# Cross-attention block: order of the first loads, products of the unit matrix at the start, and keys and scaling in the first unit

## The chip, the cores and the metric

The kernel runs on one core of one Trainium2 chip. The metric is the device time of one execution in microseconds (us). Before the change it is 1689.89 us, the median of three runs that lie between 1689.68 and 1690.12. One more execution was recorded with the profile; all durations below come from it.

## The reference

Three residual blocks on x (8 x 64 rows of 512). Only the first one is touched. It is a cross-attention from x to a context of 8 batches x 1601 keys x 256:

```python
q = (layernorm(x) @ Wq).reshape(B, Sq, 16, 128)    # Wq 512 x 2048
k = (ctx @ Wk).reshape(B, Skv, 16, 128)            # Wk 256 x 2048
v = (ctx @ Wv).reshape(B, Skv, 16, 128)
q, k = rmsnorm(q, gq), rmsnorm(k, gk)              # over each head's 128
attn = softmax(einsum('bqhd,bkhd->bhqk', q, k) / sqrt(128))
x = x + einsum('bhqk,bkhd->bqhd', attn, v).reshape(B, Sq, 2048) @ Wo
```

Behind it come a causal self-attention and a feed-forward block with ternary weights.

## The kernel before

**Scores without stored keys.** The scores are not computed from keys that lie in memory. Wk is folded into the queries: for each head a = Wk_h^T (q gq gk) is made once (`a_sb`), so a score is a product of the raw context with a. The root of each key's mean square (its rmsnorm) is still needed, and for that the keys are computed, squared and summed, but not kept. Every product on TensorE (PE) is in fp32, and a matmul instruction of fp32 shows as two records in the profile.

**Units and steps.** There are 16 units u = (b, g): 8 batches, 2 groups of 8 heads. A batch's 1601 keys are 12 tiles of 128 and a rest of 65, the *tail*. `step(u, q)` handles two tiles, q = 0 to 5. The key product of two tiles and the score product are each made from seven block products instead of eight (the names p_u, p_5, p_2 and c12, c22, c11 belong to the keys' blocks, s_a and s_2 to the scores'). The order on PE, VectorE (DVE), ScalarE (ACT) and GpSimd (POOL) is the order in which the Python code calls them; only SyncE's transfers are placed by a scheduler. In one step:

- p_u (a11 b11), copied to p1 by ACT (L917); then the early part of tail work, if any; then the scaling of the step before (`later`, L931-932); in q5 the tail's scores sp (L633);
- p_5 and s_a, copied to p5 and half (L944, L951); p_u again, copied to u2 (L956); p_5 again; c12 = p_5 + u2 on DVE (L963) and its four squares with sums on ACT (`squares`, L684);
- on DVE a transpose of the next context blocks (`transpose_context`, L194) (in unit 0 in steps q1 to q4); on ACT and DVE some work on the feed-forward weights (L597 to L612);
- `product_7`: p_u a third time and c22 = p_u + p5 on DVE (L981), its squares on ACT;
- two s_a, DVE's sum L1006, p_2, c11 (L1010) and its squares; the late part of the tail work; the fourth p_u product (a22 n4), which adds onto the bank that c22 has read, and its squares on ACT; s_2 and the last s_a.

`scale_pair` is put into `later` at the end of a step: Ln and Exp on ACT (L104, L105: the root of sixteen sums), a DVE product that scales the 128 x 1024 scores (L654), and DVE's running maxima (L668, L670; one for the first pair of tiles, two for each other pair).

From u = 1 on, a step also holds the softmax and the value products of the unit before (`weigh`, L775), which unit 0 does not have.

**Tails.** All 8 x 65 tail keys are laid side by side in `cxP` and cut into five tiles. `tail_roots` / `key_roots` (L260 to L290) make their key products kp (L266, two halves of 4 heads for each tile and group; each half is two matmuls 128x512), squares on ACT (L274), sums on DVE (L275), and the root; then small DMAs put it in its place. For g = 0 this is done at the very start, for g = 1 in unit 0: one tile in each of q0 to q3, a half early and a half late in the step (the fifth tile's roots are made before).

**The start.** `load_tails` (L252 to L257) loads the tails in four pairs of batches, 133 KB each: b0-1 and b4-5 on SyncE's queue, b2-3 and b6-7 on ScalarE's. Then SyncE's queue loads the first half of Wk for g = 0 (524 KB; columns 0 to 511 of both row blocks, L301), its second half, x in four tiles (262 KB each, L312), Wq and the rest; ScalarE's queue loads gq and gk (L315, L316). POOL makes the unit matrix `ident`. PE turns the tails of four batches by transposes (`turn_tails`, L507), then makes kp with Wk's first half for each tile, the second halves, the turned rows of x, the queries (`two_heads`) and a. Unit 0 begins at 126.69 us.

Of the kernel before, what the change touches and what calls it, by code (L numbers as in the profile page):

```python
# [1 line left out]

# [7 lines left out]
F32 = mybir.dt.float32  # L10
# [9 lines left out]
P = 128  # L20
# [8 lines left out]
def perceiver_kernel(  # L29
# [18 lines left out]
    nc = tc.nc  # L48
# [3 lines left out]
    HD = gq.shape[0]  # L52
# [3 lines left out]
    HG = H // G  # L56
# [3 lines left out]
    NC = C // P  # L60
    NJ = (KV + P - 1) // P
    TAIL = KV - (NJ - 1) * P
# [15 lines left out]
    const = ctx.enter_context(tc.tile_pool(name="const", bufs=1))  # L78
# [5 lines left out]
    ident = const.tile([P, P], F32, name="ident")  # L84
# [61 lines left out]
    wk_sb = [wkv.tile([P, NC, HG * HD], F32, tag="w", name=f"wk{g}") for g in range(G)]  # L146
# [100 lines left out]
    cxP = const.tile([P, NC, B, TAIL], F32, name="cxP")  # L247
    krP = const.tile([P, B, H], F32, name="krP")

    def load_tails(qp):  # L250
        t = qp.tile([P, B, C], F32, tag="wq3", name="cxt")
        for b in range(0, B, 2):  # L252
            (nc.scalar if b % 4 else nc.sync).dma_start(
                t[:TAIL, b : b + 2], cx[b : b + 2, NJF * P :, :].rearrange("b k c -> k b c")
            )
        return t

    def key_roots(ct, g, kr, new_kp, new_ksq):


        r = kr.shape[0]
        ssq = small.tile([P, HG], F32, tag="ssq", name="ssq", bufs=5)
        for p in range(HG // 4):
            kp = new_kp()
            for c in range(NC):
                nc.tensor.matmul(  # L266
                    kp[:r].rearrange("p h d -> p (h d)"),
                    ct(c),
                    wk_sb[g][:, c, ts(p, 4 * HD)],
                    start=(c == 0),  # L270
                    stop=(c == NC - 1),
                )
            ksq = new_ksq()
            nc.scalar.activation(ksq[:r], kp[:r], AF.Square)  # L274
            nc.vector.tensor_reduce(ssq[:r, ts(p, 4)], ksq[:r], AX.X, ALU.add)  # L275
            yield
        rsqrt_into(kr, ssq[:r], 1.0 / HD, eps_t)

    def tail_roots(i, g, new_kp, new_ksq):

        flat = cxP.rearrange("p c b k -> p c (b k)")
        n0, n1 = i * P, min((i + 1) * P, B * TAIL)
        kr = small.tile([P, HG], F32, tag="krt", name="krt", bufs=5)[: n1 - n0]
        yield from key_roots(lambda c: flat[:, c, n0:n1], g, kr, new_kp, new_ksq)

        for b in range(B):
            a, e = max(n0, b * TAIL), min(n1, (b + 1) * TAIL)
            if a < e:
                nc.sync.dma_start(
                    krP[a - b * TAIL : e - b * TAIL, b, ts(g, HG)], kr[a - n0 : e - n0, :]  # L290
                )

    n_tails = (B * TAIL + P - 1) // P
    with tc.tile_pool(name="qphase", bufs=1) as qp, tc.tile_pool(
        name="qps", bufs=2, space=PSUM
    ) as ps:
        cxt = load_tails(qp)

        def load_wk(g, p):
            cols = slice(4 * HD * p, 4 * HD * (p + 1))  # L300
            nc.sync.dma_start(  # L301
                wk_sb[g][:, :, cols],
                wk[:, g * HG * HD : (g + 1) * HG * HD][:, cols].rearrange(
                    "(c p) n -> p c n", p=P
                ),
            )

        for p in range(HG // 4):
            load_wk(0, p)
        x_sb = qp.tile([P, NTT, D], F32, tag="x_sb", name="x_sb")  # L310
        for t in range(NTT):
            nc.sync.dma_start(x_sb[:, t, :], xf[ts(t, P), :])  # L312
        gq_t = const.tile([P, 1], F32, name="gq_t")
        gk_t = const.tile([P, 1], F32, name="gk_t")
        nc.scalar.dma_start(gq_t, gq.rearrange("(p o) -> p o", o=1))  # L315
        nc.scalar.dma_start(gk_t, gk.rearrange("(p o) -> p o", o=1))  # L316
        wq_sb = []

        def load_wq(i):
# [12 lines left out]
            load_blocks(0, q)  # L332

        xT = qp.tile([P, ND, NT], F32, name="xT_q")
        gqk = const.tile([P, 1], F32, name="gqk")
        wkT, qraw, qr = {}, {}, {}

        def transpose_wk(h):
# [150 lines left out]
        with tc.manual_schedule(  # L489
            engines={  # L490
                mybir.EngineType.PE,
                mybir.EngineType.DVE,
                mybir.EngineType.Activation,
            }
        ):

            roots = [
                tail_roots(i, 0, new_kp, new_ksq_) for i in range(n_tails)
            ]
            xns_q = []  # L500

            def turn_tails(n):
                nonlocal n_b
                while n_b < n:
                    tp = ps.tile([P, NC, P], F32, tag="q", name="tp_cx", bufs=3)
                    for c in range(NC):
                        nc.tensor.transpose(  # L507
                            tp[:, c, :TAIL],
                            cxt[:TAIL, n_b, ts(c, P)],
                            ident[:TAIL, :TAIL],  # L510
                        )
                    (nc.scalar.copy if n_b % 2 else nc.vector.tensor_copy)(
                        cxP[:, :, n_b, :], tp[:, :, :TAIL]
                    )
                    n_b += 1


            ends = [-(-min((i + 1) * P, B * TAIL) // TAIL) for i in range(n_tails)]
            n_b = 0
            turn_tails(ends[0] + 2)  # L520
            mvs = []
            for i in range(n_tails):
                if i == 2:
                    mvs = [moments(x_sb, t) for t in range(2)]
                    xns_q = [normalise(x_sb, t, qp, mvs[t]) for t in range(2)]
                next(roots[i])
                turn_tails(min(ends[min(i + 1, n_tails - 1)] + 2, B))
            nc.vector.scalar_tensor_tensor(
                gqk, gq_t, float(HD) ** -0.5, gk_t, ALU.mult, ALU.mult
            )  # L530
            load_wq(3)
            for i in range(n_tails):
                if i == NTT:
                    row_sums()
                next(roots[i], None)
                if i < NTT:
                    tp = ps.tile([P, ND, P], F32, tag="tp", name="tp_ln")
                    for c in range(ND):
                        nc.tensor.transpose(tp[:, c, :], xns_q[i][:, ts(c, P)], ident)
                    nc.scalar.copy(xT[:, :, ts(i, P)], tp)  # L540
                    if i + 2 < NTT:
                        xns_q.append(normalise(x_sb, i + 2, qp))
                    next(roots[i], None)
            head_sums(0)
            for n in range(H // 2 + 1):
                if n + 1 < H // 2:
                    head_sums(n + 1)
                two_heads(n)
                if n == 0:
                    next(roots[NTT], None)  # L550
                if n == HG // 2:
                    weight_sums(0)
                    transpose_context(0, 0)

    ps = ctx.enter_context(
        tc.tile_pool(name="ps", bufs=2, space=PSUM, reuse_waits="tile")
    )
# [124 lines left out]
    def squares(ssq, half, k):  # L682
        for h in range(4):
            nc.scalar.activation(  # L684
                k[:, ts(h, HD)],
                k[:, ts(h, HD)],
                AF.Square,
                accum_out=ssq[:, 4 * half + h : 4 * half + h + 1],
            )
# [190 lines left out]
    later = []  # L880

    def weigh(k):
        nonlocal n_av
        for _ in range(k):
# [4 lines left out]
                    finish(n_av // NJ)  # L889
            n_av += 1  # L890

    def step(u, q):
        nonlocal n_tp, n_q, wv_sb
        b, g = divmod(u, G)
# [23 lines left out]
        roots = iter(())  # L918
        if u > 0:
            weigh(1)  # L920
        elif q < n_tails - 1:
            roots = tail_roots(
                q,
                1,
                lambda: ps.tile([P, 4, HD], F32, tag=f"y{q % 2}", name="kp", bufs=1),
                new_ksq,
            )
            next(roots)
        for js in probs[1:]:
            less_max(u - 1, js)  # L930
        while later:  # L931
            later.pop(0)()

        n_early = 1 if q == 4 else 0
# [27 lines left out]
        c12 = kept("c12")  # L962
        nc.vector.tensor_tensor(c12, p_5, u2, ALU.add)  # L963
        squares(ssq[:, 0], 1, c12)
        for js in probs[n_early + 1 :]:
            exponentials(u - 1, js)
        if probs:
# [69 lines left out]
            scale_scores(u, q, s, kr)  # L1037

        later.append(scale_pair)
        if u == 0 and q == n_tails - 2:  # L1040
            weight_sums(1)
        if q == NQU - 1 and u < last:
            query_sums(u + 1)
# [278 lines left out]
    with tc.manual_schedule(engines={mybir.EngineType.PE}):  # L1322
# [115 lines left out]
        o = own_projection(2)  # L1438
# [13 lines left out]
        o = own_projection(3)  # L1452
# [63 lines left out]
        for t in range(NTT):  # L1516
            op = ps.tile([P, D], F32, tag="m", name="fop")
            y = t2([P, D], "fy")

            n_parts = 2 if t == NTT - 1 else 1  # L1520
            for part in range(n_parts):
                cols = ts(part, D // n_parts)
                for r in range(NF):
# [3 lines left out]
                    for n_ in range(2):  # L1527
# [4 lines left out]
                            start=(r == 0 and n_ == 0),  # L1532
                            stop=(r == NF - 1 and n_ == 1),
                        )
                if t == 0:
                    ss = ps.tile([P, NTT], F32, tag="y0", name="ss", bufs=1)
                    for k in range(NTT):
# [4 lines left out]
                            start=True,  # L1542
                            stop=True,
# [55 lines left out]
```

## Time and profile before

| what | us |
|---|---|
| median of three runs | 1689.89 |
| profiled execution | 1689.57 |
| its span, first to last instruction | 1687.8 |
| PE busy in the span | 1668.6 |
| DVE, ACT, POOL busy | 1194.6, 1155.2, 448.1 |
| first record of PE / first kp | 3.77 / 9.60 |
| unit 0, steps q0 to q5 | 126.69 to 199.96 |

The profile is that of one execution on the chip. Its page gives the busy time of each engine, and "the chain that ended last", which is followed back from the last instruction: at each step to what released it. Besides, the trace can be asked for the waits of an engine (who waited for whom, how long), for the timeline of an engine (start, duration, engine, line, operation, tiles, number of records taken together; in brackets the idle time before it and what ended it), and for windows of time (busy time of each engine, the granted clock, the share of the DMA engines that was busy, and GB/s). Matmuls are pipelined: the spacing of the records, not the duration of one, says what a product costs PE. A 128x512 product of fp32 follows the next after 0.86 us in the full-speed parts of the trace.

### The profile page before, as it was taken

What the parts mean: (1) busy time and instruction counts of PE and PEld (TensorE: products, weight loads), DVE (VectorE), ACT (ScalarE), POOL (GpSimd) and SP (SyncE); (2) the same over time, 40 slices, a digit from 0 to 9 for tenths busy, and PEclk for the clock granted to TensorE, in tenths of its full rate; (3) what the DMA queues carried; (4) which work ended last, traced back from release to release, by engine and by line L of the source; (5) the groups of instructions that cost most, each with busy time, mean ns of one, the idle gap of its engine ahead of it and who ended that gap; (6) DMA issues with size and microseconds to landing.
All of it is one profiled execution on the core that took longest, in us unless ns stands there. A gap on an engine that the chain in (4) does not pass through costs nothing.

```text
span 1687.8 us, 20130 instructions
## 1 busy us (share of the span) xinstructions
PE 1668.6 (99%) x5472; PEld 953.1 (56%) x5472; DVE 1194.6 (71%) x1918; ACT 1155.2 (68%) x4511; POOL 448.1 (27%) x590
## 2 busy tenths in 40 slices
PE   7999899999999999999999999999999999999999
PEld 4665455555555555555555555555555554466787
DVE  4446878787888778787878787878788786245541
ACT  4667787878787877777777878787878773023441
POOL 3211232324232323232322323242324122100040
PEclk9999999999999999999999999999999999999999
DMA  6001122212221222222222222121221216500330
GB/s 200 16 0 36 33 52 45 48 39 50 49 52 36 45 47 49 48 43 47 43 49 47 44 46 47 40 57 43 46 43 37 63 30 238 156 1 1 100 101 25
DMA packets 255977, 92.61 MB, mean 55 GB/s; under 512 B 210144, under 2 KB 236536, under 8 KB 255864
## 3 DMA queue, kind: packets, MB, share of 16 engines
q1 hardware_dynamic: 246426, 69.04, 18.3%
q0 software_dynamic: 8864, 22.02, 4.4%
q8 instruction: 43, 0.70, 0.2%
q14 instruction: 70, 0.57, 0.1%
q10 hardware_dynamic: 574, 0.27, 0.1%
HBM read 77.62 MB, written 7.34 MB: 50 GB/s over the span
## 4 chain that ended last, share of the span: by engine, by line
PE 94%; ACT 3%; DVE 2%; DMA 1%; issue 0%; SPq 0%; DVEq 0%; ACTq 0%
PE y L775 21%; PE p_u L680 19%; PE s_a L680 14%; PE p L680 14%; PE gu L1414 4%; PE op L861 3%; PE s L680 2%; PE fop L1528 2%; PE mm_qk L1209 2%; PE aps L484 2%; PE vp L846 2%; PE sp L633 2%; PE q_u L388 2%; PE kp L266 1%; PE q L388 1%; ACT c L684 1%
## 5 line engine op out<-in xcount | busy, mean ns | idle before, releaser
L684 ACT ACTIVATE c<-c 128x128 f32<-128x128 f32 x1152 | 340.6, 297 | 143.4 <-DVE c L981 57.7
L775 PE MATMUL y<-s,cxn 128*128 128x512 f32 x768 | 356.6, 592 | 0.0
L775 PEld LDWEIGHTS y<-s,cxn 128*128 128x128 f32 x768 | 144.6, 190 | 151.2 <-issue 137.0
L684 ACT ACTIVATION_READ_ACCUMULATOR c<-c 128x1 f32 x1152 | 215.4, 187 | 0.0
L762 POOL TENSOR_TENSOR den<-den,s 128x512 f32<-128x512 f32 x150 | 190.7, 1271 | 43.4 <-ACT s L753 36.4
L680 PEld LDWEIGHTS s_a<-aT,cxS 128*128 128x128 f32 x576 | 109.3, 190 | 138.0 <-issue 126.8
L969 POOL COPY gate<-mx 128x1 f32<-128x1 f32 x60 | 11.0, 183 | 619.0 <-DVE mx L668 287.6
L680 PE MATMUL s_a<-aT,cxS 128*128 128x256 f32 x576 | 171.4, 379 | 0.0
L654 DVE TENSOR_TENSOR s<-s,ssq 128x1024 f32<-128x1024 f32 x96 | 117.2, 1221 | 25.4 <-ACT ssq L105 25.3
L753 ACT ACTIVATE s<-s,zero_t 128x1024 f32<-128x1024 f32 (+1 forms) x117 | 115.9, 991 | 4.6 <-DVE s L749 4.6
L670 DVE TENSOR_TENSOR mx<-mx,s 128x512 f32<-128x512 f32 x160 | 113.6, 710 | 7.5
L749 DVE TENSOR_TENSOR s<-s,mB 128x1024 f32<-128x1024 f32 (+1 forms) x117 | 116.4, 1017 | 2.2 <-ACT mB L727 2.1
L981 DVE TENSOR_TENSOR c<-p_u,p 128x512 f32<-128x512 f32 x96 | 64.9, 676 | 71.6 <-PE p_u L680 71.6
L1006 DVE TENSOR_TENSOR s<-s_a,half 128x512 f32<-128x512 f32 x96 | 66.1, 688 | 58.1 <-POOL den L762 40.7
L684 ACT ACTIVATE p_u<-p_u 128x128 f32<-128x128 f32 x384 | 99.9, 260 | 9.4
L680 PE MATMUL p_u<-wkS,cxT 128*128 128x512 f32 x192 | 98.7, 595 | 2.3 <-DVE c L981 2.3
L680 PE MATMUL p_u<-wkS,cxS 128*128 128x512 f32 x192 | 98.3, 594 | 1.5 <-ACT p L917 1.5
L680 PE MATMUL p<-wk,cxS 128*128 128x512 f32 x192 | 98.4, 594 | 0.0
L680 PE MATMUL p<-wkS,cxS 128*128 128x512 f32 x192 | 98.1, 592 | 0.0
L680 PE MATMUL p<-wk,cxT 128*128 128x512 f32 x192 | 98.0, 592 | 0.0
L680 PE MATMUL p_u<-wk,cxS 128*128 128x512 f32 x192 | 98.0, 592 | 0.0
L680 PE MATMUL p_u<-wk,cxT 128*128 128x512 f32 x192 | 98.0, 592 | 0.0
(232 smaller groups left out, 3248.4 us busy)
## 6 DMA issues: line engine op xcount, KB each, us to landing
cxn<-in_ctx_dram SPq DMA_DIRECT2D x192, 128.0 KB
cxB<-in_ctx_dram SPq DMA_DIRECT2D x192, 64.0 KB
wf<-in_L_ffn_w_gate_up_dram SPq DMA_DIRECT2D x32, 256.0 KB
fgu<-fw POOLq DMA_DIRECT2D x4, 2048.0 KB, 8.9
fw<-wT SPq DMA_DIRECT2D x192, 32.0 KB
wq<-in_L_xattn_Wq_dram SPq DMA_DIRECT2D x4, 1024.0 KB
wf<-in_L_ffn_w_proj_dram SPq DMA_DIRECT2D x16, 256.0 KB
wo<-in_L_xattn_Wo_dram POOLq DMA_DIRECT2D x16, 256.0 KB, 6.9
```

Of the source, the lines that this page charges most:

```text
L388: nc.tensor.matmul(out_, a[:, c], b[:, c], start=first, stop=True, skip_group_check=not first)
L654: nc.vector.tensor_tensor(flat, flat, kr.unsqueeze(2).to_broadcast([P, 2 * HG, S]), ALU.mult)
L670: nc.vector.tensor_tensor(mx[u][:r], mx[u][:r], s[:r], ALU.max)
L680: nc.tensor.matmul(out_, a, w, start=start, stop=True, skip_group_check=not start)
L684: nc.scalar.activation(k[:, ts(h, HD)], k[:, ts(h, HD)], AF.Square, accum_out=ssq[:, 4 * half + h : 4 * half + h + 1],)
L749: nc.vector.tensor_tensor(t, t, m.to_broadcast([r, len(js), W]), ALU.subtract)
L753: nc.scalar.activation(t, t, AF.Exp, bias=zero_t[: t.shape[0]], scale=1.0)
L762: eng.tensor_tensor(den[u][:r], den[u][:r], s[:r], ALU.add)
L775: nc.tensor.matmul(yps[u][c], cxn[u, j][:r, ts(c, P)], s[:r], start=(j == 0), stop=(j == NJ - 1),)
L981: nc.vector.tensor_tensor(c22, p_u, p5, ALU.add)
L1006: nc.vector.tensor_tensor(quarters[:, 1::2], s_a, half[:, 0:2], ALU.add)
L1414: nc.tensor.matmul(gu[:, cols], fgu_sb[rr // 8][:, rr % 8, c, :], xs_[n_][c][:, cols], start=(c == 0 and n_ == 0), stop=(c == ND - 1 and n ...
```

## The change

It has three parts.

1. *First loads.* SyncE's queue now starts with tails b0-1, Wk's first row block (columns 0 to 511), tails b4-5; ScalarE's with tails b2-3, Wk's second row block, tails b6-7. The other half of Wk is loaded as before by L301's line, but DVE first writes one column of its place (a copy out of tail b2-3, a memset and two small copies), and the load has to wait for these writes; on SyncE it now stands behind the first three tiles of x. gq and gk are loaded through POOL's queue; gq's load stands between the two instructions that make the unit matrix.
2. *Unit-matrix products.* PE multiplies the unit matrix with itself three times (128x256) before the first transposes of the tails and three times after them. Their result is not used.
3. *Unit 0.* The tail keys of g = 1 are handed out in halves from one chain over the four tiles: q0, q1 and q4 take two (early and late), q2 and q3 one (early), q5 none. In unit 0 alone, the scaling of the step before is called behind c12 and its squares, instead of ahead of p_5. The sums of Wk's blocks for g = 1 (`weight_sums(1)` on POOL) move from the end of q3 to the end of q4.

```diff
     def load_tails(qp):
         t = qp.tile([P, B, C], F32, tag="wq3", name="cxt")
         for b in range(0, B, 2):
-            (nc.scalar if b % 4 else nc.sync).dma_start(
+            q = nc.scalar if b % 4 else nc.sync
+            q.dma_start(
                 t[:TAIL, b : b + 2], cx[b : b + 2, NJF * P :, :].rearrange("b k c -> k b c")
             )
+            if b < 4:
+                c = b // 2
+                q.dma_start(wk_sb[0][:, c, 0 : 4 * HD], wk[ts(c, P), 0 : 4 * HD])
+        nc.vector.tensor_copy(gqk[:TAIL], t[:TAIL, 3, 0:1])
+        nc.vector.memset(gqk, 0.0)
+        for c in range(NC):
+            nc.vector.tensor_copy(wk_sb[0][:, c, 4 * HD : 4 * HD + 1], gqk)
         return t
...
-        for p in range(HG // 4):
-            load_wk(0, p)
+        load_wk(0, 1)
...
-        nc.scalar.dma_start(gq_t, gq.rearrange("(p o) -> p o", o=1))
-        nc.scalar.dma_start(gk_t, gk.rearrange("(p o) -> p o", o=1))
+        nc.gpsimd.dma_start(gq_t, gq.rearrange("(p o) -> p o", o=1))
+        nc.gpsimd.dma_start(gk_t, gk.rearrange("(p o) -> p o", o=1))
...
+            idle = ps.tile([P, 2, P], F32, tag="ss", name="idle", bufs=1)
+            def idle_products(n):
+                for _ in range(n):
+                    nc.tensor.matmul(
+                        idle, ident, ident.unsqueeze(1).to_broadcast([P, 2, P]),
+                        start=True, stop=True,
+                    )
+            idle_products(3)
             turn_tails(ends[0] + 2)
+            idle_products(3)
...
+    roots_1 = itertools.chain(
+        *(tail_roots(i, 1, new_y, new_ksq) for i in range(n_tails - 1))
+    )
     def step(u, q):
...
-        elif q < n_tails - 1:
-            roots = tail_roots(
-                q,
-                1,
-                lambda: ps.tile([P, 4, HD], F32, tag=f"y{q % 2}", name="kp", bufs=1),
-                new_ksq,
-            )
-            next(roots)
+        elif q < n_tails:
+            roots = itertools.islice(roots_1, 0 if q in (2, 3) else 1 if q < 2 else None)
+            next(roots_1)
...
-        while later:
+        while later and u > 0:
             later.pop(0)()
...
         nc.vector.tensor_tensor(c12, p_5, u2, ALU.add)
         squares(ssq[:, 0], 1, c12)
+        while later:
+            later.pop(0)()
...
-        if u == 0 and q == n_tails - 2:
+        if u == 0 and q == n_tails - 1:
             weight_sums(1)
```

More of the change, by code (lines that the diff above doesn't have):

```diff
@@ L1 @@
+import itertools
 from contextlib import ExitStack
@@ L248, in perceiver_kernel @@
     krP = const.tile([P, B, H], F32, name="krP")
+    gqk = const.tile([P, 1], F32, name="gqk")
     def load_tails(qp):
@@ L334, in perceiver_kernel @@
         xT = qp.tile([P, ND, NT], F32, name="xT_q")
-        gqk = const.tile([P, 1], F32, name="gqk")
         wkT, qraw, qr = {}, {}, {}
@@ L519, in perceiver_kernel @@
             n_b = 0
+            idle = ps.tile([P, 2, P], F32, tag="ss", name="idle", bufs=1)
+            def idle_products(n):
+                for _ in range(n):
+                    nc.tensor.matmul(
+                        idle,
+                        ident,
+                        ident.unsqueeze(1).to_broadcast([P, 2, P]),
+                        start=True,
+                        stop=True,
+                    )
+            idle_products(3)
             turn_tails(ends[0] + 2)
+            idle_products(3)
             mvs = []
@@ L890, in weigh, with new_y @@
             n_av += 1
+    n_y = 0
+    def new_y():
+        nonlocal n_y
+        n_y += 1
+        return ps.tile([P, 4, HD], F32, tag=f"y{n_y % 2}", name="kp", bufs=1)
+    roots_1 = itertools.chain(
+        *(tail_roots(i, 1, new_y, new_ksq) for i in range(n_tails - 1))
+    )
     def step(u, q):
```

## The prediction

> **What bounds the kernel now.** I read the engine totals and the chain first, then TensorE's waits up to 200 us (the start and unit 0 of the attention, the only places the change touches), then the timelines there.
>
> ```profile
> span 1687.8 us, 20130 instructions
> PE 1668.6 (99%) x5472; PEld 953.1 (56%) x5472; DVE 1194.6 (71%) x1918; ACT 1155.2 (68%) x4511; POOL 448.1 (27%) x590
> PE 94%; ACT 3%; DVE 2%; DMA 1%; issue 0%; SPq 0%; DVEq 0%; ACTq 0%
> ```
>
> TensorE (PE) is busy all but 19 us: the time changes by PE's gaps, by work added to PE, and by PE running at a lower clock. Nothing else counts.
>
> ```profile
> PE kp L266 <- DMA wk<-in_L_xattn_Wk_dram: 4.5, 1, 4.5
> PE tp_cx L507 <- DMA cxt<-in_ctx_dram: 3.8, 1, 3.8
> PE p_u L680 <- DVE c L981: 1.9, 2, 1.3
> PE p_u L680 <- ACT p L917: 0.6, 1, 0.6
> ```
>
> Two groups of gaps: 8.3 us before the first key product (columns: sum, times, longest), and in unit 0 small ones, most on c22 (L981). PE's timeline of the start shows a third cost, a slow clock:
>
> ```profile
> 3.77 1.32 PE L507 MATMUL tp_cx<-ident,cxt 65*128 65x65 f32 x8 [3.77 <-DMA cxt<-in_ctx_dram]
> 9.60 3.65 PE L266 MATMUL kp<-wk,cxP 128*128 128x512 f32 x4 [4.50 <-DMA wk<-in_L_xattn_Wk_dram]
> ...
> 13.33 1.93 PE L266 MATMUL kp<-wk,cxP 128*128 128x512 f32 x4
> ```
>
> A matmul of fp32 is two records. The same four take 3.65 us at 9.60 and 1.93 at 13.33 (the last record's tail of about 0.2 included): half speed until about 13.0, which is 3.4 us after PE's steady work began. From 13.08 PE has 1.4 us of gaps up to unit 0 at 126.69, so what the start gains is carried almost rigidly.
>
> **The start.** The change brings half of Wk's first half to both queues behind two key pairs, not four. Before, PE needs the 1056 KB of tails and first Wk piece; after, cxt 0 to 3 and the two Wk pieces, 266 + 524 = 790 KB. The transfers are what limits:
>
> ```profile
> 2.00:4.00 2.00, 0.23 (x2) 0.26 (x3) 0.00 (x0) 0.04 (x1) 0.00 (x0) 1.00 0.86 233
> 6.00:8.00 2.00, 0.00 (x0) 0.00 (x0) 0.00 (x0) 0.00 (x0) 0.00 (x0) 1.00 0.80 249
> ```
>
> (last two columns: share of the DMA engines, GB/s). At 233 to 258 GB/s from 2 us on, 790 KB are there at 5.3 us. The first Wk piece lay ready on most engines at 6.8 though PE waited until 9.60: by the completion records two engines ended 2 to 2.7 us after the rest. So the halves come between 5.3 and 6.6, or with the same laggards at 7.7 to 9.0. The later loads are not due: second Wk half at 21.4, x at 16.7, each landed 5 us or more before; holding one by a DVE write costs PE nothing, though if the hold reached past 18 us PE would wait there one for one. On SP the held load stands before x's fourth tile and the Wq loads; Wq's sums are used at 34.3. The four tiny DVE writes stand before the copies of tp_cx and wait for cxt 2-3, which tp_cx waits for too (landed by 4.0).
>
> gq and gk go from ACT's queue to POOL's, and gq's issue stands ahead of the unit matrix's last step. Such an issue on POOL takes
>
> ```profile
> 1398.05 0.54 POOL L840 DMA_DIRECT2D wo<-in_L_xattn_Wo_dram  x1 [0.67 <-PE y L775]
> 1412.21 0.76 POOL L1096 DMA_DIRECT2D wa_qk<-in_L_attn_w_attn_dram  x1 [13.63 <-DVE o_h L857]
> ```
>
> so ident is ready at 1.9 to 2.4 us instead of 1.32 (1.03 + 0.29). PE then runs three unit products 128x256: each half of a cold 128x512 matmul of 2 x 0.854 us (spacing of the records at 9.60), so 3 x 0.854 = 2.56, to 4.5-5.0; transposes 0.9 to 1.1 (1.32 for eight records at the same clock, less where it rises), to 5.5-6.0. The clock rises 3.4 us after 1.9-2.4, i.e. at 5.3-5.8, so the last three products take 1.29 (warm; to 6.8-7.3) or 2.56 (cold; to 8.1-8.6). Key products start when both are done: 6.8 to 9.0; I take 7.9, the middle. They take 4 x 0.43 = 1.72 warm, ending at 9.6, where before the next work began at 13.08: **-3.5 us**. Bounds: start 6.8 warm gives 8.5, -4.6; start 9.0 cold gives 9.0 + 3.4 = 12.4, -0.7.
>
> The Trainium skill, "TensorE: Matmul & The Clock Gate", section "Part 1: The HAM clock gate (the 'warmup' mystery)", says that the window of about 3.4 us runs free and doesn't start with the kernel's work; the row above, 3.4 us, fits a start on its edge. By that rule the warm clock could come up to one window later than I take, and some of the gain with it. The skill's "DMA: Bandwidth & Descriptors", section "Issuing engines are not separate DMA queues", speaks against loading by two queues: it says this saves issue time only. The 0.80 to 0.94 shares agree that the engines are the limit; here what comes first changes, not the rate, so by rule and by row the gain is that of order alone.
>
> **Unit 0, keys.** The eight halves of L266 (1.72 us each) are only spread anew: two in q0, q1 and q4, one in q2 and q3; before two in q0 to q3. PE's work stays: six steps of 9.03 plus 9 x 1.72 (sp included) = 69.7 us. Before the steps took 12.46, 12.46, 12.47, 12.64, 10.82, 12.42 = 73.3, so 3.6 us of stalls, in q4 and q5:
>
> ```profile
> 185.71 1.12 PE L680 MATMUL p_u<-wkS,cxT 128*128 128x512 f32 x2 [0.54 <-DVE c L981]
> 198.13 1.12 PE L680 MATMUL p_u<-wkS,cxT 128*128 128x512 f32 x2 [1.32 <-DVE c L981]
> ```
>
> That is the product a22*n4, which adds onto the bank that c22 reads. Spreading keys alone would help q4.
>
> **Unit 0, scaling.** Before, the scaling of step q-1 (two ACT steps, a DVE product of 1.22, one or two maxima, one in q1) runs early in step q. After it stands behind c12 and its squares: ahead of cxT and of **c22 on DVE**, and ahead of c22's squares on ACT. DVE in step q1 (from 139.15) before:
>
> ```profile
> 143.59 1.22 DVE L654 TENSOR_TENSOR s<-s,ssq 128x1024 f32<-128x1024 f32 x1
> 144.84 0.69 DVE L668 TENSOR_TENSOR mx<-s 128x512 f32<-128x512 f32 x1
> 145.45 0.68 DVE L963 TENSOR_TENSOR c<-p,u 128x512 f32<-128x512 f32 x1
> 146.05 0.70 DVE L194 STREAM_TRANSPOSE cxT<-cxB 128x512 f32<-128x512 f32 x1
> 146.67 0.67 DVE L981 TENSOR_TENSOR c<-p_u,p 128x512 f32<-128x512 f32 x1
> ```
>
> c12 keeps its time, since PE up to there is unchanged. Its four squares run on ACT from 146.17 to 147.38, offsets 7.02 to 8.22. Then Ln and Exp:
>
> ```profile
> 142.82 0.33 ACT L104 ACTIVATE ssq<-ssq,eps_t 128x16 f32<-128x16 f32 x1
> 143.18 0.31 ACT L105 ACTIVATE ssq<-ssq,zero_t 128x16 f32<-128x16 f32 x1
> ```
>
> 0.67 together, to 8.89; scaling from 8.99 to 10.2; a maximum to 10.9, a second to 11.6; cxT to 12.25 (one maximum to 11.55); c22 to 12.9 (12.2). PE reaches a22*n4 at 9.03, or at 10.75 with a late key half before it (early half or sp included). So it stalls: q0 nothing (no scaling yet), q1 12.2 - 10.75 = 1.4, q2 and q3 3.9 each, q4 12.9 - 10.75 = 2.2, q5 3.2 (no cxT; up to 4.2, since DVE work beside POOL was slower there, the scaling 1.57 against 1.22). Steps: 12.5, 13.9, 14.65, 14.65, 14.6, 13.95 = 84.2, **+11.0** on 73.3. The first step of unit 1 has 1.8 us of stalls on the same chain; its scaling stays early, I take 0.5 back. The moved sums on POOL (one step later) are first used in unit 1. Bounds for the unit: +8 if DVE's and ACT's steps overlap more than in these rows or the transposes hide, +12.5 with POOL's slowdown in q4 and q5.
>
> **Sum.** 1689.57 (profiled execution; span 1687.8, 1.8 lie around it) + 11.0 - 0.5 - 3.5 = 1696.6; the median, 1689.89, stands 0.3 above it, so **1696.9 us**.
>
> **Rivals.**
> - (a) *c22 doesn't bind*: in the rows c22 is done at 8.2 and wanted at 9.03 or 10.75, and the start gain stands. If moving the scaling delays c22 by less than 0.8 us (DVE not blocked by the wait for ACT), keys in halves also remove the 3.6 us: 1689.57 - 3.5 - 3.6 = 1682.5. Against: engines run in order, and c22 comes after the scaling in program order. 7%.
> - (b) *The start pays for a smaller loss*: -4.6 and +6 to +8, 1691 to 1693. 10%.
> - (c) *No gain at the start*: the loads behind (x on SP is issued without a wait) share the engines, the laggards stay, ident is late: 1689.57 + 10.5 = 1700.1. 14%.
> - (d) *Unit products don't raise the clock* (the change doesn't do what it says): key products at 7.9 take 3.4, end 11.3, -1.8: 1698.3. 11%.
> - My forecast: 58%.
>
> About 0.2% (3.4 us) can be told from no change here. Faster: (a), 0.07. Same: (b) and a small tail of the forecast, 0.11. Slower: 0.82. Range 1691.0 to 1701.5: from (b) with both best bounds to +12.5 with -0.7.
>
> **What would show it.** Right: PE's waits up to 200 us list c22 (L1017 now) with about 14 us in five of unit 0's six steps, q2 and q3 the longest near 3.9; DVE shows scaling between c12 and c22 in unit 0; kp begins near 7.9 with four records in 1.9 us; unit 0 begins near 123.2. Wrong: step q2 of about 10.8 us (then (a)), first kp records of 3.6 us (d), or kp at 9.6 again (c).

## The result, and the profile after

The changed kernel takes 1702.54 us (median of four runs, 1700.53 to 1704.03), against 1690.01 before: 1.0078 times, interval 1.0066 to 1.0090. It is slower, as forecast, but by 12.5 us instead of 7.0, and it lies outside the range. The execution with the profile took 1700.53, the least of the four: its span, PE's busy time and the waits of PE up to 230 us (columns: sum, times, longest):

```profile
span 1698.7 us, 20159 instructions
PE 1674.5 (99%) x5484; PEld 957.5 (56%) x5484; DVE 1195.8 (70%) x1922; ACT 1156.6 (68%) x4511; POOL 448.5 (26%) x592
```

```profile
PE p_u L707 <- DVE c L1017: 14.0, 6, 3.6
PE idle L537 <- POOL ident masks.py:199: 2.5, 1, 2.5
```

The two waits for transfers at the start (8.3 us) have become one of 2.5 us for the unit matrix; the waits for c22 have grown from 2.3 (three of them up to 230 us) to 14.0 us. PE is busy 5.9 us longer. The six added products take some 4.2 of it (2.46 to 5.18 and 6.26 to 7.72), the first key products give back 1.8, and 3.5 are left: part of PE's work ran slower. PE's timeline of the start:

```profile
2.46 2.93 PE L537 MATMUL idle<-ident 128*128 128x256 f32 x6 [2.46 <-POOL ident masks.py:199]
5.18 1.29 PE L519 MATMUL tp_cx<-ident,cxt 65*128 65x65 f32 x8
6.26 1.62 PE L537 MATMUL idle<-ident 128*128 128x256 f32 x6
7.72 1.88 PE L280 MATMUL kp<-wk,cxP 128*128 128x512 f32 x4
```

Key products begin at 7.72 instead of 9.60 and take 1.88 instead of 3.65. Unit 0 begins at 122.98 instead of 126.69: 3.71 us gained. It ends at 210.92 and takes 87.94 instead of 73.27: 14.67 lost. The difference, 10.96, is all of the profiled execution's loss. PE's wait for c22 in q1 to q5, with the wait in brackets:

```profile
147.87 1.12 PE L707 MATMUL p_u<-wkS,cxT 128*128 128x512 f32 x2 [1.52 <-DVE c L1017]
...
162.48 1.12 PE L707 MATMUL p_u<-wkS,cxT 128*128 128x512 f32 x2 [3.60 <-DVE c L1017]
...
178.79 1.12 PE L707 MATMUL p_u<-wkS,cxT 128*128 128x512 f32 x2 [3.60 <-DVE c L1017]
...
193.39 1.30 PE L707 MATMUL p_u<-wkS,cxT 128*128 128x512 f32 x2 [1.88 <-DVE c L1017]
...
209.10 1.12 PE L707 MATMUL p_u<-wkS,cxT 128*128 128x512 f32 x2 [3.00 <-DVE c L1017]
```

They are 1.5, 3.6, 3.6, 1.9, 3.0 = 13.6 us (the sixth wait is in unit 1), where the forecast had 1.4, 3.9, 3.9, 2.2, 3.2. And DVE in q2 shows why, as the walk had it: c12, then 1.9 us idle for the root, the scaling, two maxima, the transpose, and only then c22:

```profile
155.98 0.69 DVE L997 TENSOR_TENSOR c<-p,u 128x512 f32<-128x512 f32 x1 [1.20 <-PE p L707]
158.55 1.22 DVE L681 TENSOR_TENSOR s<-s,ssq 128x1024 f32<-128x1024 f32 x1 [1.88 <-ACT ssq L106]
159.81 1.42 DVE L697 TENSOR_TENSOR mx<-mx,s 128x512 f32<-128x512 f32 x2
161.15 0.70 DVE L195 STREAM_TRANSPOSE cxT<-cxB 128x512 f32<-128x512 f32 x1
161.77 0.65 DVE L1017 TENSOR_TENSOR c<-p_u,p 128x512 f32<-128x512 f32 x1
```

Waits of 13.6 us on 69.7 of work make 83.3; unit 0 took 87.94. What is missing stands in the clock. Windows of 3.41 us, laid from the moment at which PE's clock first rose, 6.48 us (columns that matter: window, its length and PE's busy time; PEclk is the number before the last two):

```profile
160.08:163.49 3.41, 1.01 (x3) 0.53 (x4) 3.38 (x6) 1.03 (x7) 1.48 (x4) 1.00 0.32 81
163.49:166.91 3.42, 3.42 (x8) 2.03 (x7) 2.45 (x7) 3.10 (x19) 0.26 (x1) 0.50 0.47 75
...
173.73:177.14 3.41, 1.46 (x5) 0.57 (x3) 2.21 (x3) 1.06 (x6) 0.00 (x0) 1.00 0.00 0
177.14:180.56 3.42, 1.77 (x6) 1.22 (x7) 2.97 (x6) 1.79 (x12) 1.74 (x4) 1.00 0.20 32
...
190.80:194.21 3.41, 1.53 (x4) 0.49 (x3) 3.38 (x6) 0.84 (x6) 1.29 (x4) 1.00 0.28 77
194.21:197.62 3.41, 3.41 (x7) 1.87 (x6) 1.58 (x4) 2.62 (x15) 3.33 (x4) 0.50 0.49 77
```

Twice a window in which PE was busy for 1.0 or 1.5 us is followed by a whole window at half clock. Each costs up to 1.7 us: 3.4 together; the rest is some 0.25 us around each wait, which the waits' list doesn't count (the records' ends are modelled, and the first product behind a wait takes 0.1 longer). The first of the two falls behind a wait of 3.6 us, the second behind one of 1.88 us only, while the other wait of 3.6 us (175.2 to 178.8) is cut in two by the windows' edge and brings nothing on. In the four runs the mean clock is 0.998, 0.997, 0.997 and 0.996, in the order of their times but for 0.6 us between the two at 0.997: each 0.001 is 1.7 us, one window at half clock. So the number of such windows varies, by these means from two to four. That this alone spreads the times isn't shown: the kernel before has a clock of 1.000 in every run and still spreads from 1686.77 to 1690.92 (16 runs beside e1 to e4), and in e4 the lowest clock, 0.996, stands beside the shortest time.

### The profile page after: what moved, and what is told of

Its sections match the earlier page's. It is cut to its first block, busy times and chain, and to the rows that moved or that the text cites. A ratio compares the mean times of both kernels' runs of the same rounds, so it can differ in the third digit from the quotient of the medians.

```text
span 1698.7 us, 20159 instructions
## 1 busy us (share of the span) xinstructions
PE 1674.5 (99%) x5484; PEld 957.5 (56%) x5484; DVE 1195.8 (70%) x1922; ACT 1156.6 (68%) x4511; POOL 448.5 (26%) x592
## 4 chain that ended last, share of the span: by engine, by line
PE 94%; ACT 2%; DVE 2%; issue 0%; DMA 0%; POOL 0%; DVEq 0%; POOLq 0%
PE y L802 20%; PE p_u L707 19%; PE s_a L707 14%; PE p L707 14%; PE gu L1450 4%; PE op L888 3%; PE s L707 2%; PE fop L1564 2%; PE mm_qk L1245 2%; PE aps L496 2%; PE vp L873 2%; PE sp L660 2%; PE q_u L400 2%; PE kp L280 1%; PE q L400 1%; PE bp L111 1%
```

## The theories

**Theory 1.** The scaling behind c12 delays c22, because DVE works in order; the waits this makes on PE cost their own length and, where they leave a window nearly empty, half clock for the next one. The start and the keys in halves are gains that stand. **Rivals:** the keys in halves or POOL's moved sums bear part of the loss; the low clock has another source; late scaling costs wherever it is put; the start's gain comes from the unit products and not from the loads. All times below have the same kernel before beside them (medians 1689.83, 1689.16 and 1689.87 in three groups: e1 to e4, e5 to e8, e9 to e11). The second group ran on another chip, so runs of different groups are compared by how far each lies from its own group's median.

## The experiments

**e1: scaling early again.** In the changed kernel:

```diff
-        while later and u > 0:
+        while later:
             later.pop(0)()
...
         squares(ssq[:, 0], 1, c12)
-        while later:
-            later.pop(0)()
```

> The changed kernel, but with unit 0's scaling in its old place (ahead of p_5); loads, unit products and keys in halves stay. Theory 1 (the whole loss is made by the scaling behind c12: 14.0 us of waits for c22, and two or more stretches of 3.4 us at half clock that these waits bring on): no waits for c22 in q1 to q4, clock 1.000 from the start's end on, 1690.0 - 3.7 at the start - 1.5 to 3.5 in unit 0 = 1683 to 1685. Rival (keys in halves or POOL's later sums carry part of the loss): above 1687.

Measured: 1684.99 us, ratio 0.9971 (0.9960 to 0.9983), clock 1.000; waits for c22 0.8 us in all, the other waits of unit 0 small:

```profile
PE p_u L707 <- DVE c L1015: 0.8, 2, 0.4
```

The place of the scaling alone is worth 1702.54 - 1684.99 = 17.5 us; the rest of the change is a gain of 4.8. The rival about keys and POOL's sums falls.

**e2: the waits filled.** PE gets work that nobody reads, where it would wait:

```diff
+        if u == 0 and q:
+            fill = ps.tile([P, 4 * HD], F32, tag=f"y{(n_y + 1) % 2}", name="fill", bufs=1)
+            for _ in range((0, 1, 4, 4, 2, 3)[q]):
+                product(fill, a11, b11, True)
         product(p_u, a22, n4, False)
```

> The changed kernel with 14 more products 128x512 that nobody reads, put on PE just ahead of a22*n4 in unit 0: 1, 4, 4, 2, 3 in q1 to q5 (0.86 us each, 12.0 us), inside the waits for c22. Theory 1 (a wait of 2 us or more brings PE down to half clock for 3.4 us, 1.7 us each time; how often depends on when the waits fall): the waits are filled, the clock stays at 1.000, unit 0 takes 84 to 85 us, 1690.0 - 3.7 + 11.0 = 1697.3, and the runs lie within 1 us of each other. Rival (the slow stretches and the spread have another source, such as the transfers or the first unit products): 1701 to 1704 as before, with the clock at 0.996 to 0.998.

Measured: 1699.47 (1698.65 to 1699.98), ratio 1.0055 (1.0042 to 1.0069), clock 1.000 in all five runs. With 12 us *more* work on PE the kernel is 3.1 us *faster* than the changed one: its slowest run lies below the changed kernel's fastest. The clock is the proof, more than the spread, which went from 3.5 to 1.3 us in few runs: with the waits filled no run has a low clock. So the low clock comes from the waits. The number was missed by 2.2: key products began at 8.36 here (clock up at 7.8), 0.6 later than in the changed kernel's profile, and in q5 a new wait of 1.2 us appeared, sp for DVE's last sum of the scores; the changed kernel's profile doesn't have it, and PE was at half clock there from 194 to 198 us.

**e3: the start alone** (unit 0 as before).

> The kernel before with the change's start alone (loads on two queues, held half of Wk, gq and gk on POOL's queue, unit products); unit 0 as before. Theory: the start's gain is carried whole to the end: 1690.0 - 3.7 = 1686.3, unit 0 at 123.0. Rival (it is given back behind, in unit 0's waits or the later loads): 1688 or more.

Measured: 1687.21 (1686.18 to 1687.55), ratio 0.9984 (0.9975 to 0.9992). A gain of 2.6, not 3.7: PE's clock rose at 8.33 us instead of 6.48, so the last unit products ran at half clock and key products began at 8.63. Unit 0 began at 123.92 and what was gained there stayed. The profiled run of the changed kernel had a lucky start.

**e4: late scaling alone**, on the kernel before (the two places of e1's diff, the other way).

> The kernel before with unit 0's scaling behind c12 alone; start and keys as before. By the walk of the prediction the waits for c22 are 1.5, 1.9, 1.9 (late key half in q1 to q3), 3.6 (q4, no keys), 3.0 (q5): 12 us, against some 3 us of waits before, so +9.4 = 1699.4 if the clock stays up. Theory 1: q4 and q5 and by chance one of the others bring on half clock, 1.7 us each: 1701 to 1705, with a clock of 0.996 to 0.999. Rival (no clock effect): 1699 to 1700 with a clock of 1.000.

Measured: 1704.98 (1703.85 to 1706.07), ratio 1.0089 (1.0075 to 1.0103), clock 0.996 to 0.998. Waits for c22 of 1.16, 1.88, 1.88, 3.59 and 3.00, three windows at half clock (behind q2, q4 and q5). The longest wait moved to q4, which has no key half here, as the walk says. Late scaling costs 15.1 us with the old keys and 17.5 with the new: with one key half instead of two, q2 and q3 have less work to put into the wait (13.6 us of waits for c22 there, 11.5 here).

**e5: gq and gk back on ScalarE's queue**, in e1's kernel.

```diff
-        nc.gpsimd.dma_start(gq_t, gq.rearrange("(p o) -> p o", o=1))
-        nc.gpsimd.dma_start(gk_t, gk.rearrange("(p o) -> p o", o=1))
+        nc.scalar.dma_start(gq_t, gq.rearrange("(p o) -> p o", o=1))
+        nc.scalar.dma_start(gk_t, gk.rearrange("(p o) -> p o", o=1))
```

> The kernel with the scaling early (changed start, keys in halves), and gq and gk back on ScalarE's queue, behind its three loads. Theory of the start (key products begin when the unit products end, and these begin when the unit matrix is there, 2.46 us because gq's issue of 0.70 us stands ahead of it on POOL): the unit products begin at 1.35, key products 1.1 us earlier on average, between 6.5 and 8.0 by where PE's clock goes up: 1685.0 - 1.1 = 1683.9. Rival (the Wk halves land only at 7 to 8, and gq's small packets hold them up): PE then shows a wait for wk, 1685 or more.

Measured: 1684.89 (1682.94 to 1685.45), ratio 0.9973 (0.9962 to 0.9984): no difference to e1 that can be told. The unit products did begin at 1.38, 1.1 us earlier, but the clock rose only at 8.82 in the profiled run, later than in e1 (8.38), and key products waited behind six unit products until 8.17. The expectation failed on the clock, not on the queue.

**e6: no unit products**, in e1's kernel (both calls of `idle_products` away).

> The kernel with the scaling early, without the six unit products. It shows when the Wk halves land: PE's wait for wk ends there. Theory: at 5.5 to 6.6; the key products then begin at half clock, which lasts until the end of the first window of 3.4 us that PE filled, 3.4 to 6.8 us later, and loses 1.7 to 3.4: 6.0 + 2.5 = 8.5 in place of 8.66, so 1685.0 within 1 us: the unit products only pay for themselves. Rival (the unit products make most of the start's gain): 1687 or more, with key products near 9.

Measured: 1684.20 (1683.64 to 1684.71), ratio 0.9971 (0.9961 to 0.9982), the same as e1.

```profile
3.99 1.50 PE L519 MATMUL tp_cx<-ident,cxt 65*128 65x65 f32 x8 [3.99 <-DMA cxt<-in_ctx_dram]
5.45 3.75 PE L280 MATMUL kp<-wk,cxP 128*128 128x512 f32 x4
```

Key products begin at 5.45 without any wait for wk: by the transfers' completion records the first row block had landed by 5.32 and the second, which is needed only from the third record on (7.29), by 5.93. They run at half clock (3.75 us for four records), until 9.9 us. In e1 the unit products hold them up until 8.66 and they run at full clock: six unit products pay for themselves and no more. The rival falls: the start's gain is there with the loads alone (this kernel lies 5.0 us below the kernel before, e11, with the old start, 2.5).

**e7: old order of the loads, with unit products**, in e1's kernel.

```diff
-            if b < 4:
-                c = b // 2
-                q.dma_start(wk_sb[0][:, c, 0 : 4 * HD], wk[ts(c, P), 0 : 4 * HD])
...
-        load_wk(0, 1)
+        for p in range(HG // 4):
+            load_wk(0, p)
```

(the four DVE writes go too).

> The kernel with the scaling early and unit products, but the tails and Wk loaded in the old order (four pairs of tails, then Wk's first half whole on one queue; nothing held). Theory (order of the loads lets key products begin at 7.7 to 8.7 instead of 9.1 to 9.6): PE waits for wk until 9.1 to 9.6, at full clock by then: 1685.0 + 0.9 = 1685.9. Rival (loads were never the matter, only the clock): 1685.0 or less, no wait for wk.

Measured: 1686.41 (1685.03 to 1688.25), ratio 0.9986 (0.9977 to 0.9994). PE waits 0.96 us for wk, until 8.64; in the profiled run the clock rose at 5.95, early, so nothing else held it. The wait ended earlier than the 9.1 to 9.6 expected. With unit products the loads' order is worth 2.1 us: e1 lies 4.8 us below the kernel before, this kernel 2.7. The two slowest of its eleven runs (1688.20 and 1688.25) show a clock of 0.999; they have no trace, and where they lost it stays open.

**e8: scaling later still**, behind c11 and its squares, in the changed kernel.

```diff
         squares(ssq[:, 0], 1, c12)
-        while later:
-            later.pop(0)()
...
         squares(ssq[:, 0], 0, c11)
+        while later:
+            later.pop(0)()
```

> The changed kernel with unit 0's scaling behind c11 and its squares, so behind c22 too: later still than in the changed kernel. Theory 1 (what costs is not that the scaling is late, but that it stands ahead of c22 on DVE): c22 is done by offset 8.2 again, no long waits, clock 1.000, 1685.0 within 1.5. Rival (late scaling costs by itself, by scores held longer or by a later wait for the sum of the scores): 1690 or more.

Measured: 1692.93 (1691.69 to 1693.36), ratio 1.0021 (1.0012 to 1.0031), clock 0.997 to 0.998. Theory 1 holds for c22 alone; the rival's time came, by one of the two ways that it named. c22 has left the list of waits, and steps q1 to q4 show hardly a wait: its place behind the scaling was the cause there. But two new waits stand in the list:

```profile
PE sp L660 <- DVE s L1054: 4.5, 1, 4.5
...
PE tp_mx L760 <- DVE mx L697: 2.4, 1, 2.4
```

The scaling in q4 now stands ahead of the sum L1054 that frees the scores' bank, and sp, the tail's scores in q5, waits 4.5 us for that bank; in unit 1 the last scaling makes the maximum late. Windows at half clock follow both (189.6 to 193.0 and 210.0 to 213.5). Late scaling needs not one free place but one in each step.

**e9: waits filled in part.** As e2 with 0, 3, 3, 1, 2 products.

> The changed kernel with 9 products that nobody reads ahead of a22*n4 in unit 0: 0, 3, 3, 1, 2 in q1 to q5, so that waits of about 1.5, 1.0, 1.0, 1.0 and 1.3 us are left, none near 2. Theory 1 (half clock follows a window of 3.4 us with about 2 us or more without work, never a shorter gap): the clock stays at 1.000 although 5 to 6 us of waits for c22 stay in the trace; 1697.3 to 1699.5, as with all waits filled. Rival (any gap in unit 0 may bring it on): slow stretches of 3.4 us again, 1700 or more.

Measured: 1699.00 (1698.56 to 1700.29), ratio 1.0054 (1.0041 to 1.0068). The waits are there, and the clock is up throughout:

```profile
PE p_u L707 <- DVE c L1017: 6.3, 6, 1.5
```

```profile
core 0: 1697.8 us, clock 1.000
```

The same time as with all waits filled, and the same clock, with 4.3 us more of waiting left in the trace (6.3 against 2.0). What sets both apart from the changed kernel is the clock. That a gap of 2 us is the bound isn't shown: no window here holds less than 2.1 us of work, and in the changed kernel a wait of 1.88 us was enough. Unit 0 takes 85.96 us here: 83.3 of work and waits (what the fillers take lies in the waits), 1.2 for sp in q5, and some 0.25 us around each wait. The wait of sp comes with the keys: on DVE the sum that it needs stands behind the sums of q4's late key half (e1, with the same keys and no late scaling, has 0.6 us of it). This is the price of late scaling at full clock, with these keys.

**e10: three unit products, ahead of the tails only**; e5's kernel without the second `idle_products(3)`.

> The kernel with the scaling early, gq and gk on ScalarE's queue, and only the first three unit products: from 1.4 to 3.9 us, while PE would wait for the tails until 4.0 anyway. Theory: they delay nothing and can only bring the clock up earlier than without any (1684.2), by up to 2 us of half clock, 0.5 us on average: 1683.7; key products begin at 5.5. Rival (transposes and the wait after them keep the window from counting, so that the clock comes up as late as without): 1684.2.

Measured: 1682.28 (1681.84 to 1684.57), ratio 0.9958 (0.9945 to 0.9970).

```profile
1.37 2.93 PE L537 MATMUL idle<-ident 128*128 128x256 f32 x6 [1.37 <-POOL ident masks.py:199]
...
5.59 1.96 PE L280 MATMUL kp<-wk,cxP 128*128 128x512 f32 x4 [0.33 <-ACT cxP L524]
```

In the profiled run the clock rose at 4.33, and key products began at 5.59 at full speed: the products lie where PE would wait anyway, and hold up nothing. It has the lowest median of all the versions, 7.6 us below the kernel before, though its runs reach into those of e6. The two intervals overlap, and the profiled run is the fastest of the five, so that it beats e6 (5.0 below) is likely, not shown.

**e11: keys in halves alone**, on the kernel before.

> The kernel before with the keys in halves alone (and POOL's later sums): start and scaling as before. Theory (it removes most of the waits in q4, 1.8 us, and some in q5): 1689.5 - 2.2 = 1687.3, the difference between the changed start alone and the kernel with the scaling early. Rival (it gains only together with the new start): 1689 or more.

Measured: 1687.38 (1685.84 to 1688.48), ratio 0.9985 (0.9976 to 0.9993): a gain of 2.5, as expected, with c22's waits at 0.8 us. In the profile unit 0 takes 71.21 us instead of 73.27, and the spread keys put a new wait of 0.6 us on sp in q5.

## Why the prediction was wrong

- **The direction, and the mechanism of the waits,** were right. The waits for c22 came to 13.6 us in unit 0 where 14.6 were worked out, each step within 0.3 us. DVE's order was read correctly from the rows.
- **The step that failed** is the sum of unit 0, "+11.0", with its upper bound of +12.5: "TensorE is busy all but 19 us: the time changes by PE's gaps, by work added to PE, and by PE running at a lower clock." I named the lower clock and then did not ask what my own gaps of 3.9 us would do to it. Unit 0 cost 14.67 in the profiled run, of which 12.7 would have been there at full clock (e9: 85.96 - 73.27). In the median the clock is worth 1702.54 - 1699.00 = 3.5 us, more than half of the 5.6 by which the forecast was missed. The sum put this term at nothing without a reason.
- Of the 12.7, 11.0 was forecast. The rest is the wait of sp (1.2), for which the sum has no term, and the short run-up behind each wait. Unit 1's first step gave back the 0.5: its second p_u begins 2.92 us behind the unit's start instead of 3.45. By the end of the program this is gone again, for reasons that the runs don't show.
- **The start**: -3.5 forecast, -3.71 in the profiled run, -2.6 on its own in the median of e3. I took the middle of 6.8 to 9.0 for the first key product; in five of the six profiles with this start it was 8.4 to 8.8, because the unit matrix was late (2.46) and the clock rose at 7.8 to 8.7. I had it rise 3.4 us after the first product, as in the kernel before; it rose 4.0 to 6.2 us after, by where the windows lay. There the key products happened to begin with a window (9.59 to 13.01); in e4, with the same loads, the clock rose 5.0 us after the first key product (9.07 to 14.04). The kernel before's profile also had its Wk late, at 9.60 (e11 7.68, e4 9.07), so the -3.71 has luck at both ends. By the completion records the last of the Wk halves landed at 5.9 to 8.0 in the nine profiles with the new order, about what I gave, and no profile shows PE waiting for them; I did not see that the unit products, put there to raise the clock, would then hold up the work itself.
- **Keys in halves** helped as forecast: -2.5 (e11), of the 3.6 us of stalls that I had read in unit 0.
- Rival (a), 1682.5, is within 2.5 us of what the kernel gives when the scaling doesn't move (e1: 1685.0). Rival (c) came near in time, 1700.1, for a wrong reason; (d) fell: the clock did rise under the unit products.

The Trainium skill, "TensorE: Matmul & The Clock Gate", section "HAM oscillation — how this bites in real kernels", gives the rule that PE should have no idle gap over about 3.4 us. Here a gap of 1.88 us was enough (the window 190.80 to 194.21 and the one in e4 before 167.64), and one of 3.60 was not always: how much work a window holds decides, not the gap's length alone (the bound, and an exception, stand below).

## What to carry to other kernels

Where an engine is full, a wait that is put into its stream must be priced twice: by its length, and by what a window left less than half full does to the clock behind it. Before an operation is moved on an engine that works in order, write down what stands behind it in its new place and by when each of these is wanted; "later" was harmless for the scores and fatal for c22. Work that is there only to raise the clock belongs where the engine would wait anyway, not ahead of work whose data may already have come: six such products gained nothing over none (e1, e6).

## What the runs showed of the hardware

- PE's clock is decided in windows of 3.413 us that run on from the first rise: 6.48 + 46 x 3.413 = 163.49, + 9 x 3.413 = 194.21 in the changed kernel; 14.04 + 45 x 3.413 = 167.64, + 9 and + 5 more windows to 198.36 and 215.42 in e4. Each time it stayed at one half for exactly one window. The windows run on to the end of the program: in e3 the clock falls at 8.33 + 491 x 3.4133 = 1684.27, behind a window with 1.11 us of work.

```profile
1680.86:1684.27 3.41, 1.11 (x10) 0.90 (x8) 0.48 (x1) 0.00 (x0) 0.00 (x0) 1.00 0.11 38
1684.27:1685.43 1.16, 0.00 (x0) 0.00 (x0) 0.00 (x0) 0.00 (x0) 0.00 (x0) 0.50 0.00 0
```

- In the profiles of the changed kernel, e4, e8 and e9, half clock followed windows, ahead of the program's end, in which PE was busy 0.00, 0.66, 1.01, 1.01, 1.37, 1.53 and 1.53 us of 3.41; it did not follow windows with 1.59, 1.62, 1.65, 1.77 or more, nor one with 1.46. The bound lies near 1.5 us; the exception shows that busy time by the profile isn't quite what is counted, and what is, stays open.
- A rise needs more than a fall leaves: in e1 the window up to 4.97 held 2.5 us of unit products (2.46 to 4.97) and the clock stayed at one half until 8.38. In e8 2.78 us (1.82 to 5.24) didn't raise it either; 2.84 in e11 (7.11 to 10.52) and 2.96 in e10 (0.92 to 4.33) did. Here too there is an exception: 3.25 us in e5 (1.99 to 5.40), about 1.1 of it transposes of 65x65, didn't.
- The profile's clock column read 1.00 for the half-speed records of the start; there only the spacing of the records shows the clock.
